# Two sequences' input rows and three sequences' output rows move by indirect DMAs from GpSimd, in a four-stage block on one core

## The chip, the core and the metric

The program runs on one core of a Trainium2 chip. The core has five instruction queues that run side by side: TensorE (PE), VectorE (DVE), ScalarE (ACT), GpSimd (POOL) and SyncE (SP), which here does nothing but issue DMAs. The metric is the device time of one execution in microseconds (us), the median of several runs; lower is better. Each engine works its own instructions off in the order in which they were written, and waits where one of them needs a result that isn't there.

## The reference

The input x is four sequences of 512 tokens with 256 features each. Four layers follow each other; each normalises x, computes something of it and adds that to x:

```python
x = L0_attn_a_x                                   # (4, 512, 256), float32
x = x + _L0_attn_a_ref(_layernorm(x), ...)        # stage m: convolution, then a selective scan over 512 tokens
x = x + _L0_ffn_ref(_layernorm(x), ...)           # stage e: 8 experts, the best two of each token weighed, RMS norm
x = x + _L0_attn_b_ref(_layernorm(x), ...)        # stage s: state-space layer of 64 heads, in chunks of 32 tokens
x = x + _L0_ffn_ref(_layernorm(x), ...)           # stage f: the expert layer again, same weights
return x
```

What matters for the change is only where x comes from and where it goes: all of x is read from the chip's memory (HBM) at the start, it stays in the on-chip memory (SBUF) through all four stages, and the sum after the last stage is written back. All numbers are float32.

## The kernel before

**Tiling.** A sequence of 512 tokens lies in SBUF as 128 partitions x 4 blocks x 256 features: the tile `x[b]` is `[P, NT, D]` with P = 128 and NT = 4, and token `i*128 + p` of sequence b is row p of block i. So one sequence is 512 KB, and each of its blocks 128 KB, 1 KB in each partition. There are four such tiles, one for each sequence, and they are never moved.

**Stages.** Within a stage the sequences follow each other, and the stages overlap at their seams: while the scans of the last sequence run, the expert layer of the first has begun, and so on. By the trace the stage of the scans (m) takes some 340 us, the expert layer (e) and the state-space layer (s) lie between 250 and 735 us, and the last expert layer (f) ends the run.

**The order of the work** is not the order of the Python code. All operations are noted first, as nodes with their inputs and outputs, by `Plan.note`. `price` gives each node a cost. `Plan.order` then simulates the engines: at each step it takes, on the engine that can start soonest, the node with the lowest rank among those that could start within 0.1 us of the earliest. `Plan.backward` gives the ranks: it schedules everything from the end backwards, and a node's rank is the latest time at which it may start by that. `Plan.issue` does both 24 times, replays each order with two sets of randomly lengthened costs, and keeps the order with the shortest replay. Then the instructions are written out in that order, all from line 611. So a change of one node's engine or cost may move any other instruction. Three details bear on the change: a DMA may not be issued more than 80 us ahead of its rank (`lead`); a DMA occupies its issuing queue for a fraction of a microsecond and a modelled transfer engine for its bytes at 360 GB/s (`Plan.run`, line 500); and the end that the replay minimises is the last instruction's end on its engine, without the landing of a DMA.

**The start.** `load(b)` (line 755) reads a sequence with one DMA of 512 KB from SP's queue. Sequence 0 is loaded first, then the weights of stage m come, sequences 1 to 3 between them. GpSimd meanwhile writes the constants: the identity `ident`, masks, `spread`, `less_all` and others, by memsets and selects. `measured(b)` (line 1174) computes the mean and variance of each row of `x[b]` on DVE (`st_m`, `mv_m`), and GpSimd raises the variance to the power -0.5 (`scale_m`).

**The end.** In stage f, `experts` (line 975) computes the experts of one block of 128 tokens: TensorE multiplies into `ph_f`, DVE adds the bias, ACT applies silu, DVE and ACT weigh the results into `cm_f`, `c_f` and `hb_f`, and GpSimd adds these: `c_f <- c_f,hb_f` and two adds `cm_f <- cm_f,c_f`. `project` (line 1011) transposes `cm_f` on TensorE (`pc_f`) and multiplies it with the projection (`pj_f`). `finish` (line 1033) takes the inverse root of the mean square on GpSimd (`rs_yf`), multiplies on DVE, and adds the result to x: by one GpSimd add of 128x1024 for a whole sequence (sequences 0, 1 and 2), or by one DVE add of 128x256 for each block (sequence 3, whose four blocks are finished one by one). Then SP writes the finished part to `out`: one DMA of 512 KB for each of the first three sequences, four of 128 KB for the last.

Of the kernel before, what the change touches and what calls it, by code (L numbers as in the profile page):

```python
# [30 lines left out]
P = 128  # L31
B, L, D = 4, 512, 256
NT = L // P
# [174 lines left out]
class Plan:  # L208
# [29 lines left out]
    def note(self, eng, op, args, kw):  # L238
# [2 lines left out]
        n.outs, n.ins = [], []  # L241
        first = True
        for k, v in [(None, v) for v in args] + list(kw.items()):
            if not isinstance(v, bass.AP):
                continue
            if k in ("out", "accum_out") or (k is None and first):
                n.outs.append(v)
            else:
                n.ins.append(v)
            if k is None:  # L250
                first = False
# [222 lines left out]
    def run(self, n, s, clock):  # L474
# [21 lines left out]
        if n.port:  # L496

            s = max(s, clock["port_of"].get(n.eng, 0.0))
            clock["port_of"]["vector" if n.eng == "gpsimd" else "gpsimd"] = s + c
        if n.dma:  # L500
            n.end = s + 0.06
            clock[n.eng] = n.end
            t = max(n.end, clock["hwdge"])
            clock["hwdge"] = t + 0.45
            n.end = clock[n.eng] = t + 0.4
            t = max(t + 0.45 + 0.65, clock["dma"])
            clock["dma"] = n.done = t + n.cost
            return
# [66 lines left out]
            self.emit(n)  # L575

    def swap(self, v):
        if not isinstance(v, bass.AP):
# [62 lines left out]

def price(plan, n):

    n.table, n.port, n.dma = None, False, n.op == "dma_start"
    out = n.outs[0]

    def place(ap):
# [69 lines left out]
def block(ctx: ExitStack, tc: Plan, a: dict, out: bass.AP):  # L717
# [5 lines left out]
    def ctile(shape, name):  # L723
        return const.tile(shape, F32, tag=name, name=name)

    def ctile_r(shape, name):
        return const.tile(shape, F32R, tag=name, name=name)

# [23 lines left out]
    for b in range(B):  # L752
        x.append(ctile([P, NT, D], f"x{b}"))

    def load(b):
        nc.sync.dma_start(out=x[b], in_=a["x"][b].rearrange("(i p) d -> p i d", p=P))

    load(0)
# [153 lines left out]
    def moe(name, w, where, sums, biased=lambda b: (), last=False):  # L912
# [120 lines left out]
        def finish(b, y, ss, lo=0, hi=NT):  # L1033
# [2 lines left out]
                V.scalar_tensor_tensor(y[:, i, :], y[:, i, :], ry[:, i - lo : i - lo + 1], norm_w, ALU.mult, ALU.mult)  # L1036
            some = x[b][:, lo:hi, :]
            (V if last and hi - lo == 1 else G).tensor_tensor(some, some, y[:, lo:hi, :], ALU.add)
            if last:
                nc.sync.dma_start(out=out[b, lo * P : hi * P, :].rearrange("(i p) d -> p i d", p=P), in_=some)  # L1040

        def steps(seqs, ahead=False):
# [960 lines left out]
```

## Time and profile before

| what | value |
|---|---|
| median of 3 runs | 843.76 us (838.05 to 845.73) |
| profiled execution | 838.11 us, its span 836.4 us |
| TensorE clock granted, mean | 0.883 of full speed |
| PE busy | 717.4 us (86%) |
| DVE busy | 683.8 us (82%) |
| POOL busy | 525.5 us (63%), 410 instructions |
| ACT busy | 523.4 us (63%) |
| loads of x (SP, 4 of 512 KB) | issued between 1.3 and 6.2 us |
| stores of sequences 0, 1, 2 (SP, 512 KB each) | 2.9 us from issue to landing (median) |
| stores of sequence 3 (SP, 4 of 128 KB) | 1.7 us from issue to landing (median) |

The span runs from the first to the last instruction; the execution's own time is 1.7 us longer, which lies around it. Busy times are shares of the whole span; the engines take turns at being the one that everything waits for. An instruction's name in the profile is `out<-in` by the program's tile names, the letter behind the underscore is the stage (m, e, s, f), and line 611 is where all of them are written out. `SPq` is the queue of DMAs that SyncE issues. Instructions that only issue DMAs aren't counted as busy time of an engine.

### The profile page before, as it was taken

To read this page: it belongs to the slowest core of one execution; us is meant where nothing else is said; L and a number is where in the kernel's file an instruction comes from. 1 tells how busy PE (TensorE), PEld (TensorE's weight loads), DVE (VectorE), ACT (ScalarE), POOL (GpSimd) and SP (SyncE) were. 2 spreads that over 40 slices of the span, in tenths; PEclk is the share of its full clock that TensorE was granted. 3 is DMA by queue.
4 is the path that set the end of the run, shared out by engine and by line. 5 is a ranking of instruction groups with operands and counts; after the bars stand their busy time and mean duration, and the time that the engine had idled before them with its cause. 6 is when DMAs were issued, how large, how long until landed. Compare 5 with 4: busy or idle time off the path is not lost. (4 is left out here: it accounts for less than half of the span.)

```text
span 836.4 us, 16364 instructions
## 1 busy us (share of the span) xinstructions
PE 717.4 (86%) x6160; PEld 460.4 (55%) x6160; DVE 683.8 (82%) x1272; ACT 523.4 (63%) x960; POOL 525.5 (63%) x410
## 2 busy tenths in 40 slices
PE   5997887977667799899998887888979888999996
PEld 2332323312013346687886666676668666878884
DVE  5439999999999994898998569785688567699987
ACT  2777875675335685678676646727736546576764
POOL 5714776776776774755558766771962864647755
PEclk9999998977569599999998678799969967999998
DMA  7362351441252101700002553431440574000101
GB/s 231 99 201 73 101 165 38 131 144 58 84 164 79 48 7 49 282 1 0 1 1 52 119 125 63 95 77 31 104 100 15 121 289 100 2 1 1 51 1 52
DMA packets 80175, 70.18 MB, mean 84 GB/s; under 512 B 48856, under 2 KB 66200, under 8 KB 79328
## 3 DMA queue, kind: packets, MB, share of 16 engines
q1 hardware_dynamic: 78624, 67.98, 28.2%
q10 hardware_dynamic: 1472, 1.15, 0.4%
q8 instruction: 49, 0.80, 0.4%
q14 instruction: 30, 0.25, 0.1%
HBM read 51.77 MB, written 17.32 MB: 83 GB/s over the span
## 5 line engine op out<-in xcount | busy, mean ns | idle before, releaser
L611 POOL TENSOR_TENSOR hs<-hs,cb 128x1024 f32<-128x1024 f32 x64 | 153.0, 2394 | 82.3 <-DVE hs L611 62.7
L611 DVE TENSOR_TENSOR_SCAN hs<-da,bx 128x512 f32<-128x512 f32 x128 | 150.9, 1206 | 2.7 <-ACT da L611 2.2
L611 ACT ACTIVATE da<-ds,a_neg 128x512 f32<-128x512 f32 x128 | 87.6, 689 | 87.0 <-DVE hs L611 83.7
L611 PE MATMUL ys<-hs,over 128*32 128x512 f32 x256 | 75.6, 737 | 29.9 <-POOL hs L611 29.9
L611 DVE TENSOR_TENSOR bx<-us,pb 128x1024 f32<-128x1024 f32 x64 | 76.1, 1200 | 9.6 <-DMA us<-u_rows 9.3
L609 ACT ACT_TABLE_LOAD x50 | 64.2, 1283 | 0.9
L611 PE MATMUL pconv<-hh,conv 128*128 128x512 f32 x128 | 61.5, 629 | 3.0 <-DVE st_m L611 1.6
L611 POOL TENSOR_TENSOR m_s<-m_s,gm_s 128x512 f32<-128x512 f32 x32 | 45.6, 1431 | 28.3 <-ACT m_s L611 27.4
L611 ACT ACTIVATE ph_e<-ph_e 128x512 f32<-128x512 f32 x64 | 36.9, 586 | 25.3 <-DVE ph_e L611 16.6
L611 ACT ACTIVATE ph_f<-ph_f 128x512 f32<-128x512 f32 x64 | 37.1, 588 | 23.6 <-DVE ph_f L611 23.4
L611 PEld LDWEIGHTS ys<-hs,over 128*32 128x32 f32 x256 | 9.3, 116 | 68.7 <-POOL hs L611 56.4
L611 DVE TENSOR_TENSOR ph_f<-ph_f,expert_b 128x512 f32<-128x512 f32 x64 | 44.0, 692 | 2.7 <-PE ph_f L611 2.1
L611 PE MATMUL ph_e<-expert_h,xs_of_xh_e 128*128 128x512 f32 x128 | 43.8, 411 | 2.7 <-ACT c_e L611 2.7
L611 PEld LDWEIGHTS pconv<-hh,conv 128*128 128x128 f32 x128 | 24.4, 198 | 35.9 <-issue 31.0
L611 DVE TENSOR_TENSOR_SCAN starts<-decays_s_p,starts 128x1024 f32<-128x1024 f32 x16 | 39.9, 2497 | 3.7 <-ACT starts L611 3.7
L611 PE MATMUL pz_s<-x_b,m_s 128*32 128x32 f32 x2048 | 33.4, 218 | 10.4 <-DMA x_b<-x_rows_s 6.3
L611 PEld LDWEIGHTS pz_s<-x_b,m_s 128*32 128x32 f32 x2048 | 27.3, 128 | 25.8 <-issue 16.9
L611 PE MATMUL pe_s<-c_s,less 128*128 128x512 f32 x64 | 32.9, 563 | 9.5 <-DMA less<-cs_rows_s 7.8
L611 ACT COPY starts<-pst_s_p 128x512 f32<-128x512 f32 (+1 forms) x32 | 30.0, 1008 | 15.6 <-PE pst_s_p L611 15.6
L611 DVE TENSOR_TENSOR m_s<-pe_s,gm_s 128x512 f32<-128x512 f32 x32 | 21.8, 681 | 21.1 <-ACT pe_s L611 13.3
L611 PE MATMUL ph_f<-expert_h,xh_f 128*128 128x512 f32 x96 | 38.3, 399 | 0.3 <-ACT xh_f L611 0.3
L611 PE MATMUL ph_f<-expert_l,xh_f 128*128 128x512 f32 x96 | 38.4, 400 | 0.0
(389 smaller groups left out, 2153.7 us busy)
## 6 DMA issues: line engine op xcount, KB each, us to landing
ds<-d_rows SPq DMA_DIRECT2D x16, 512.0 KB, 3.8
us<-u_rows SPq DMA_DIRECT2D x16, 512.0 KB, 4.4
decays_s_p<-dk_rows_s SPq DMA_DIRECT2D x32, 256.0 KB, 4.1
cb<-c_rows SPq DMA_DIRECT2D x16, 256.0 KB, 3.5
x_rows_s<-xw_s SPq DMA_DIRECT2D x16, 256.0 KB, 2.4
x_b<-x_rows_s SPq DMA_DIRECT2D x64, 64.0 KB, 2.9
x<-in_x_dram SPq DMA_DIRECT2D x4, 512.0 KB, 7.7
raw_expert<-in_expert_w_dram SPq DMA_DIRECT2D x4, 512.0 KB, 6.4
```

The costliest lines, as they stand in the source:

```text
L609: self.real.scalar.preload_act_table_set(n.table)
L611: n.inst = f(*[self.swap(v) for v in n.args], **{k: self.swap(v) for k, v in n.kw.items()})
```

## The change

A table `tokens` of 128 x 16 integers is written by one GpSimd instruction (`iota`): column `b*4 + i` holds the token numbers `(b*4 + i)*128 + p` of block i of sequence b, counted over all 2048 tokens. Sequences 2 and 3 are then loaded by four indirect DMAs each, one for each block of 128 rows (128 KB), whose rows are named by a column of the table; and sequences 0, 1 and 2 are stored by four indirect DMAs each, again a block of 128 rows at a time. GpSimd issues all twenty. Sequences 0 and 1 are loaded, and sequence 3 is stored, by SP as before. The rows that move are the same as before. The planner learns of the new kind: such a DMA holds GpSimd for 1.3 us and begins to move data 1.0 us later.

```diff
@@ Plan.note
+            if isinstance(v, bass.IndirectOffsetOnAxis):
+                v = v.ap
@@ Plan.run
+        if n.dma and n.eng == "gpsimd":
+            n.end = clock[n.eng] = s + 1.3
+            t = max(n.end + 1.0, clock["dma"])
+            clock["dma"] = n.done = t + n.cost
+            return
         if n.dma:
@@ price
-    n.table, n.port, n.dma = None, False, n.op == "dma_start"
+    n.table, n.port, n.dma = None, False, n.op in ("dma_start", "indirect_dma_start")
@@ block
+    tokens = ctile_i([P, B * NT], "tokens")
+    G.iota(tokens, pattern=[[P, B * NT]], base=0, channel_multiplier=1)
+
+    def rows_of(b, i):
+        return bass.IndirectOffsetOnAxis(ap=tokens[:, b * NT + i : b * NT + i + 1], axis=0)
+
     def load(b):
+        if b > 1:
+            for i in range(NT):
+                G.indirect_dma_start(
+                    out=x[b][:, i, :], out_offset=None, in_=a["x"].rearrange("b t d -> (b t) d"), in_offset=rows_of(b, i)
+                )
+            return
         nc.sync.dma_start(out=x[b], in_=a["x"][b].rearrange("(i p) d -> p i d", p=P))
@@ finish
-            if last:
+            if last and hi - lo > 1:
+                for i in range(lo, hi):
+                    G.indirect_dma_start(
+                        out=out.rearrange("b t d -> (b t) d"), out_offset=rows_of(b, i), in_=x[b][:, i, :], in_offset=None
+                    )
+            elif last:
                 nc.sync.dma_start(out=out[b, lo * P : hi * P, :].rearrange("(i p) d -> p i d", p=P), in_=some)
```

The rest of the diff lets the planner's `swap` replace the table's tile inside such an argument, as it does for other tiles.

More of the change, by code (lines that the diff above doesn't have):

```diff
@@ L577, in swap @@
     def swap(self, v):
+        if isinstance(v, bass.IndirectOffsetOnAxis):
+            return bass.IndirectOffsetOnAxis(ap=self.swap(v.ap), axis=v.axis)
         if not isinstance(v, bass.AP):
@@ L724, in ctile, with ctile_i @@
         return const.tile(shape, F32, tag=name, name=name)
+    def ctile_i(shape, name):
+        return const.tile(shape, mybir.dt.int32, tag=name, name=name)
     def ctile_r(shape, name):
```

## The prediction

> **What bounds the kernel now.** I read the page's slices first, then the busy time of each engine in four stretches where the change touches GpSimd, then GpSimd's instructions in order of time at both ends, then the chain that ended last. The slices of GpSimd say that it is nowhere full.
>
> ```profile
> POOL 5714776776776774755558766771962864647755
> PEclk9999998977569599999998678799969967999998
> ```
>
> The stretches hold, after their total, the busy time of PE, weight loads, DVE, ACT and POOL, then the granted clock, the DMA share and GB/s.
>
> ```profile
> 0.00:47.00 47.00, 37.25 (x84) 14.80 (x84) 23.26 (x81) 25.92 (x41) 27.34 (x47) 1.00 0.56 173
> 640.00:700.00 60.00, 50.47 (x963) 38.82 (x961) 36.58 (x72) 32.25 (x56) 36.76 (x32) 0.82 0.64 182
> 760.00:800.00 40.00, 40.00 (x218) 33.80 (x217) 36.38 (x96) 28.20 (x69) 27.47 (x23) 1.00 0.08 27
> 800.00:837.00 37.00, 28.16 (x139) 22.83 (x138) 29.13 (x77) 20.55 (x51) 20.89 (x22) 0.93 0.09 29
> ```
>
> In the first 47 us GpSimd is busy for 27.3 and so idle for 19.7. In 760 to 800 TensorE is full (40.00 of 40), DVE has 91%, and GpSimd idles for 12.5. In the last 37 us TensorE has only 28.2: the run ends with a chain through all engines, block by block of sequence 3. From 640 to 700 TensorE idles for 9.5 us while the DMA engines are at 64%: there the weights of stage f are read back.
>
> Here is GpSimd at the very end (start, duration, tiles, and in brackets the idle time before):
>
> ```profile
> 818.66 1.29 POOL L611 TENSOR_TENSOR c_f<-c_f,hb_f 128x512 f32<-128x512 f32 x1 [1.80 <-ACT hb_f L611]
> 821.75 1.63 POOL L611 TENSOR_TENSOR cm_f<-cm_f,c_f 128x256 f32<-128x256 f32 x2 [1.80 <-DVE cm_f L611]
> 823.33 2.37 POOL L611 TENSOR_TENSOR x<-x,xnb_f 128x1024 f32<-128x1024 f32 x1
> 825.66 1.28 POOL L611 TENSOR_TENSOR c_f<-c_f,hb_f 128x512 f32<-128x512 f32 x1
> 827.01 1.55 POOL L611 TENSOR_TENSOR cm_f<-cm_f,c_f 128x256 f32<-128x256 f32 x2
> 828.52 1.09 POOL L611 TENSOR_TENSOR rs_yf<-sd_yf,minus_half 128x1 f32<-128x1 f32 x2
> 830.14 0.72 POOL L611 TENSOR_TENSOR rs_yf<-sd_yf,minus_half 128x1 f32<-128x1 f32 x1 [0.53 <-DVE sd_yf L611]
> 832.07 0.72 POOL L611 TENSOR_TENSOR rs_yf<-sd_yf,minus_half 128x1 f32<-128x1 f32 x1 [1.21 <-DVE sd_yf L611]
> ```
>
> From 821.75 to 832.79 it is hardly idle, and the chain that ended last runs through it (start, length, engine and tile):
>
> ```profile
> 823.38 2.33 POOL x L611
> 825.71 1.24 POOL c_f L611
> 827.01 0.75 POOL cm_f L611
> ```
>
> The add of 128x1024 at 823.3 is the last step of sequence 2 (`finish`). It has nothing to do with sequence 3, but sequence 3's `c_f` add stands behind it. So, at the place where sequence 2's results leave, GpSimd itself is what the end waits for. That is the one place where more GpSimd work must cost something.
>
> **What is removed.** Five DMAs leave SP's queue: two loads of x, three stores.
>
> ```profile
> L611 SPq DMA_DIRECT2D out_dram<-x x7: 332/350/400, 778.9 to 833.8; - x7
> L611 SPq DMA_DIRECT2D x<-in_x_dram x4: 368/476/507, 1.3 to 6.2; - x4
> ```
>
> At 0.35 us for a store and 0.48 for a load (the middle figures of min/median/max) that is 2.0 us of SP. At the start SP issued the loads of sequences 2 and 3 at 5.83, and `dt_w` stood behind them at 8.09; but `dt_w` is first read at 39.6, so nothing is gained by its coming 2 us earlier. At the end nothing but sequence 3's own stores stands behind sequence 2's, and these were waiting for DVE. I count 0, and at most 2.0 gained.
>
> **What is added.** One `iota`, eight gathers and twelve scatters on GpSimd's queue. No indirect DMA is in this trace. By kind the nearest row is SP's issue of the same 128 KB, 0.35 us; by engine it is GpSimd's largest piece of work, 2.4 us for 128x1024. I take 1.3: the add of 128x512 on GpSimd takes 1.29, and the new plan is computed with 1.3, so its order fits if that is right. For the landing I take the row of the stores of 128 KB, 1.7 us after the issue, and up to 8.7, the longest landing of any transfer of x. For `iota` I take the 0.3 us of a select of 128x128.
>
> *The start.* 8 x 1.3 + 0.3 = 10.7 us, against 19.7 idle before 47 us; at 2.4 it would be 19.5, just as much as there is. A gather waits for nothing but the table, so it blocks nothing behind it by waiting, only by its 1.3 us. Behind it in GpSimd's queue stand the powers `scale_m`, the first of which is on the way to the first convolution: it ended at 14.39 and DVE used it at 16.29, so 1.9 us of delay are free and one gather in front of it is covered. The rows of sequences 2 and 3 are read by DVE at about 20 us. If they come late, DVE stands still, as it works in order; before its next urgent work (`b_s` at 37.8) it had 9.1 us idle, which covers seven more microseconds of gathers. That cover is gone if one costs over 2.4 us. The same 1 MB now competes from a second queue with the convolution's weights, which TensorE awaited until 9.64. Together +0.5 us, with bounds 0 and +3 (the 1.3 us of one gather in front of a power and 1.7 for one late landing).
>
> *Sequences 0 and 1.* 8 x 1.3 = 10.4 us of GpSimd in the 40 us after 776 us or so, where it has 12.5 idle; TensorE is full there and what it multiplies next (`ph_f`) doesn't come from GpSimd, only `pc_f` does, a few times. A scatter waits for the add in front of it on the same engine, so nothing else is held up by the wait, but each may hold a `c_f` or `cm_f` add by up to 1.3 us. +1 us. Bounds: 0, and 8 x 2.4 - 12.5 = +6.7, if the issue is that long and all of the excess reaches TensorE.
>
> *Sequence 2.* 4 x 1.3 = 5.2 us. After its add ended at 825.7, GpSimd had 7.1 us to the end of its last power at 832.79, 5.4 of them busy: 1.7 are free. 3.5 are too many. Behind the last power they would put the last issue at 836.3 and its landing at 838.0, where the last store of sequence 3 was issued at 833.8 and, with 1.7 us, landed at 835.5: +2.5. But the planner may also pull sequence 2 forward: its power was ready at 813.0, DVE's multiplies of it were spread from 815.8 to 822.0, and GpSimd idled for 4.4 us between 813 and 823 (0.8 + 1.8 + 1.8). Then the add leaves the end's chain. I take +2; bounds 0 and 4 x 2.4 = +9.6.
>
> **Sum** 0 + 0.5 + 1 + 2 = +3.5, between -2.0 and +19.3. Against the profiled execution's 838.11 (span 836.4, and 1.7 around it) that is 841.6. That execution is 5.65 below the median of the runs, 843.76, so the median to expect is 847.3; I say 847. The three runs lie 0.9% apart; about 1% is what a measurement of this kernel can tell from no change.
>
> **A rule that speaks against the change.** The trace shows DVE standing still because of GpSimd:
>
> ```profile
> 23.78 2.59 DVE L611 TENSOR_SCALAR sd_m<-mv_m 128x4 f32<-128x4 f32 x4
> 23.78 2.38 POOL L611 TENSOR_TENSOR expert_l<-raw_expert,expert_h 128x1024 fp32r<-128x1024 f32 x1 [2.07 <-ACT expert_h L611]
> ...
> 39.65 0.16 DVE L611 TENSOR_SCALAR scale_m<-scale_m 128x4 f32<-128x4 f32 x1
> ```
>
> Four instructions of 128x4 take 2.59 us on DVE in the 2.38 us in which GpSimd subtracts 128x1024; later one such takes 0.16 us. The Trainium skill (SBUF — State Buffer, "Who interferes with whom") has this the other way round too: a DMA issued from GpSimd needs descriptors that GpSimd writes through the port it shares with DVE, and a DVE instruction in a two-port mode keeps it out until it ends. No transfer of this trace is issued by GpSimd, so no row shows that. By the rule gathers beside DVE's copies at the start would be the late ones; its example is 3.1 us in place of 0.62, and by that eight would be up to 20 us late (an estimate from that page). At the end DVE works mostly out of TensorE's result memory. My sum doesn't use this; it goes by the bounds above.
>
> **The rivals.**
>
> *Absorbed, a little slower* (47%): as summed, 847.
>
> *The issue is dear* (20%): a gather or scatter holds GpSimd for 2.4 us. For: an add of 128x1024 takes that long, and how long it takes to write out 128 rows' addresses no row shows. Against: the adds of 128x256, the tile that such a DMA moves, take 0.75. Then the middle costs up to 6.7, the end four times 1.1 more than above (6.4), the start 3: +16, or 860. It decides from 12.5 / 8 = 1.6 us an issue upward, where the eight no longer fit into the idle time.
>
> *The new order is worse in the middle* (21%): since one node's cost changes all ranks, the order of everything is new. The place that is sensitive is 671 to 687: 5 MB of weights were put ahead of small transfers on SP's queue, the chain has 13.4 us of `expert_h` there, and TensorE idled for 9.5 us of those 60. A like mistake once more costs some 9.5: 843.8 + 9.5 = 853. Against it: the planner tries 24 orders.
>
> *The new order is better there* (12%): the same 9.5 us won, with the 3.5 of the sum: 838. To pass the bound of 1% below it must also win the 1.3 us by which sequence 2's add held `c_f` and a little more, 835.
>
> **How the numbers follow.** 847 is the likeliest. Slower by over 1% (above 852) are the two slower cases, 41%, less the part of them that stays below: 39%. Faster by over 1% (below 835) is most of the last case, 11%. Within 1% is the rest, 50%. A range of 8 in 10 leaves out the lower half of the last case and the upper half of the dear issue: 838 to 860.
>
> **What would show it.** Right: gathers in GpSimd's gaps before 47 us and the first scan on DVE at about 63.8 us as before; TensorE still full from 760 to 800; scatters issued 1 to 1.6 us apart; the last GpSimd work after sequence 2's add 2 to 5 us longer than before. Wrong: an issue far from 1.3; DVE idle before `st_m` of sequence 3; another stretch between 60 and 760 that is longer or shorter by more than all of this, which would be the order's doing and not the DMAs'.

## The result, and the profile after

The changed kernel takes **876.03 us** (median of 4 runs, 872.16 to 877.39); the kernel before, measured beside it, 844.75 (838.05 to 845.85). The ratio is **1.038**, with a 95% interval of 1.0316 to 1.0444. The forecast was 847, its range 838 to 860. The profiled execution of the changed kernel took 876.33 us, its span is 874.6, against 836.4 before: 38.2 us more to explain. By the medians it is 31.3; the profiled execution of before was a short one, so some 7 of the 38.2 are chance.

All instructions are now written out at line 620, and everything in the middle lies some 20 us later. The page's slices of GpSimd and of the granted clock:

```profile
POOL 7814876767765675645466867547734657466755
PEclk9998999977667699899997799698688769999996
```

GpSimd is still nowhere full, so it has not become the engine that bounds the whole. The granted clock is 0.875 in the mean; before it was 0.883. The stretches answer to those of before (total; PE, weight loads, DVE, ACT, POOL; granted clock, DMA share, GB/s); the third and fourth are moved by 20 us:

```profile
0.00:47.00 47.00, 34.74 (x75) 13.95 (x75) 18.59 (x80) 20.14 (x33) 35.26 (x55) 0.96 0.51 158
660.00:720.00 60.00, 50.33 (x909) 40.04 (x909) 29.71 (x54) 30.69 (x54) 36.87 (x31) 0.78 0.65 177
780.00:820.00 40.00, 37.19 (x187) 30.80 (x186) 33.43 (x81) 24.79 (x59) 28.74 (x26) 0.96 0.05 17
820.00:875.00 55.00, 36.60 (x175) 29.03 (x174) 39.07 (x91) 25.19 (x62) 31.67 (x33) 0.84 0.08 27
```

GpSimd has 35.26 us in the first 47 instead of 27.34, which is about the eight gathers: unlike SP's issues, an indirect DMA is counted as busy time of GpSimd here (55 instructions instead of 47). The second row, around the reload of stage f's weights, has as much of TensorE as before (50.33 and 50.47 of 60). In the third row TensorE was full before (40.00 of 40); now it has 37.19. The end, 37 us before, is 55 us long, and TensorE is busy for 36.6 of it. The transfers themselves, from the profile's view of the tile `x` (duration of the issue, not of the transfer; min/median/max in ns, first and last start):

```profile
L620 POOL DMA_INDIRECT out_dram<-x,tokens x12: 960/1012/1083, 794.9 to 868.2; - x12
L620 POOL DMA_INDIRECT x<-in_x_dram,tokens x8: 947/987/1433, 1.9 to 22.2; - x8
L620 SPq DMA_DIRECT2D out_dram<-x x4: 356/370/405, 862.9 to 871.6; - x4
L620 SPq DMA_DIRECT2D x<-in_x_dram x2: 454/476/499, 1.3 to 1.8; - x2
```

An issue of an indirect DMA takes 0.99 to 1.01 us in the median. SP keeps two loads and sequence 3's four stores, at what they cost before. Twenty issues are 20 us of GpSimd, of which much had idle time to lie in; so their price is not what explains 38 us. What does, at the end, is seen in GpSimd's order of time at the end (start, duration, tiles, idle time before and what ended it):

```profile
794.92 1.08 POOL L620 DMA_INDIRECT out_dram<-x,tokens  x1 [0.17 <-POOL c_f L620]
797.70 0.96 POOL L620 DMA_INDIRECT out_dram<-x,tokens  x1 [1.70 <-DMA out_dram<-x,tokens]
...
821.80 0.99 POOL L620 DMA_INDIRECT out_dram<-x,tokens  x1
826.08 0.96 POOL L620 DMA_INDIRECT out_dram<-x,tokens  x1 [3.29 <-DMA out_dram<-x,tokens]
827.07 1.29 POOL L620 TENSOR_TENSOR c_f<-c_f,hb_f 128x512 f32<-128x512 f32 x1
...
865.40 1.04 POOL L620 DMA_INDIRECT out_dram<-x,tokens  x1 [2.94 <-DMA out_dram<-x]
868.16 0.96 POOL L620 DMA_INDIRECT out_dram<-x,tokens  x1 [1.73 <-DMA out_dram<-x,tokens]
```

The scatters don't run freely behind the add. The second started 1.70 us after the first had been issued, and the releaser is the landing of the first; the third of the next sequence waited 3.29 us for the second, and `c_f <- c_f,hb_f` stood behind it. Every scatter names the whole of `out` as its destination, since only the table says which rows it writes; so the program orders each behind the one before. The stores of sequence 3 on SP's queue write to the same tensor, and are in the same chain: the scatter at 865.40 waited 2.94 us for one of them. The waits of SP's queue for scatters are (us in all, times, the longest):

```profile
SPq L620 <- DMA out_dram<-x,tokens: 148.6, 5, 98.7
```

Five waits, the longest of 98.7 us: SP comes to a store long before its data are there, so most of this costs nothing. At the very end it does cost. The chain that ended last (start, length, what) now goes through these transfers:

```profile
862.90 1.72 DMA out_dram<-x
...
865.40 1.04 POOL out_dram L620
...
869.14 0.59 POOL rs_yf L620
```

Before, its last 13 us were GpSimd's adds and the work of other engines on sequence 3; now a store of sequence 3, a scatter of sequence 2 that waits for it, and behind the last scatter the power of sequence 3's last block, 0.59 us. After TensorE's last instruction the changed kernel runs on for 12.3 us; before it was 5.7.

Three moments that are the same work in every version cut the span into stretches: the first scan of stage m on DVE, the last product `po_s` of stage s on TensorE, and the end. By them the 38.2 us of the two profiles fall into three parts:

| stretch (us) | before | after | more |
|---|---|---|---|
| start to the first scan | 63.8 | 67.0 | +3.2 |
| first scan to the last `po_s` | 667.1 | 683.7 | +16.6 |
| last `po_s` to the end | 105.5 | 123.9 | +18.4 |

No indirect DMA lies in the middle one. So there were two questions: what do the DMAs cost where they are, and what does the new order of everything cost?

### The profile page after: what moved, and what is told of

Its sections match the earlier page's. It is cut to its first block, busy times and chain, and to the rows that moved or that the text cites. A ratio compares the mean times of both kernels' runs of the same rounds, so it can differ in the third digit from the quotient of the medians.

```text
span 874.6 us, 16387 instructions
## 1 busy us (share of the span) xinstructions
PE 728.8 (83%) x6160; PEld 463.2 (53%) x6160; DVE 685.3 (78%) x1272; ACT 533.7 (61%) x969; POOL 544.0 (62%) x431
## 4 chain that ended last, share of the span: by engine, by line
PE 35%; DVE 12%; ACT 9%; issue 4%; SPq 4%; DMA 4%; POOL 2%; POOLq 0%; ACTq 0%; DVEq 0%
PE ph_e L620 7%; PE ph_f L620 6%; SPq L620 4%; PE po_s L620 3%; DVE hs L620 3%; PE pz_s L620 3%; ACT L618 3%; PE px_s L620 2%; PE pst_s_p L620 2%; PE po_s_p L620 1%; DMA decays_s_p<-dk_rows_s 1%; PE pe_s L620 1%; DVE bx L620 1%; PE pr_s L620 1%; PE pj_e L620 1%
## 5 line engine op out<-in xcount | busy, mean ns | idle before, releaser
L620 POOL TENSOR_TENSOR hs<-hs,cb 128x1024 f32<-128x1024 f32 x64 | 150.7, 2364 | 77.6 <-DVE hs L620 61.6
L620 PE MATMUL ys<-hs,over 128*32 128x512 f32 x256 | 84.6, 781 | 34.7 <-POOL hs L620 34.7
L620 PE MATMUL pconv<-hh,conv 128*128 128x512 f32 x128 | 59.0, 603 | 2.3 <-ACT hh L620 2.3
L620 PE MATMUL pz_s<-x_b,m_s 128*32 128x32 f32 x2048 | 33.2, 209 | 12.8 <-DMA x_b<-x_rows_s 7.0
L620 PE MATMUL ph_f<-expert_h,xl_f 128*128 128x512 f32 x96 | 38.9, 405 | 0.0
```

The lines of the kernel that those rows point to most:

```text
L620: n.inst = f(*[self.swap(v) for v in n.args], **{k: self.swap(v) for k, v in n.kw.items()})
```

## Experiments: the order and the DMAs taken apart

Theory O: most of the loss is the new order. Theory D: most of it is the DMAs themselves. They can be parted, because the order is planned first and written out after: one can plan with one kind of DMA and write out the other.

**Before's order with the indirect DMAs** (`old_order_indirect`). The plan is before's, instruction by instruction on each engine; where a load of sequence 2 or 3 or a store of sequence 0, 1 or 2 comes up, four indirect DMAs are written out on GpSimd instead.

```diff
+        if "rows" in n.kw:                       # a load of 2, 3 or a store of 0, 1, 2
+            b = n.kw["rows"]
+            for i in range(NT):
+                at = IndirectOffsetOnAxis(ap=tokens[:, b*NT+i : b*NT+i+1], axis=0)
+                g.indirect_dma_start(...)        # gather into x[b][:, i, :], or scatter from it
+            return
```

> The plan of the kernel before is kept for all engines; only where it issued the loads of sequences 2 and 3 and the stores of sequences 0, 1 and 2 from SP, four indirect DMAs of GpSimd stand in GpSimd's queue instead. If the new order of everything is what costs (theory O: about 20 of the 31 us were lost before stage f began, in stretches that hold no indirect DMA): 855 to 862, the loss all in the first 50 us and after 776 us, because each block of four scatters holds GpSimd for about 4 x (1.0 issue + 1.7 wait for the scatter before) = 10.8 us and the last block stands in the end's chain. If the indirect DMAs themselves cost (theory D): 872 to 880, and the stretches between 130 and 640 us longer too.

Measured: 875.05 us (873.08 to 877.81), ratio 1.0384 (1.0316 to 1.0452). First scan at 72.5 (+8.7), middle stretch 668.1 (+1.0), end 133.8 (+28.3). The order is before's, and yet all of the loss is there. Theory D's time is met; its other half, longer stretches between 130 and 640 us, is not, as the whole middle is 1.0 us longer.

**The new order with plain DMAs** (`new_order_plain`). The plan is the changed kernel's; at each of the twenty places SP issues a plain DMA of the same 128 KB.

```diff
+        if n.op == "indirect_dma_start":
+            b, i = n.kw["rows"]
+            rows = slice(i * P, (i + 1) * P)
+            if n.kw["in_offset"] is None:
+                sync.dma_start(out=out[b, rows, :], in_=n.kw["in_"])
+            else:
+                sync.dma_start(out=n.kw["out"], in_=x[b, rows, :])
+            return
```

> The order of the changed kernel is kept for all engines; each of the twenty indirect DMAs is a plain DMA of the same 128 KB from SP. Theory O: 862 to 868 (stage f begins 20 us late as in the changed kernel, and what the scatters cost after that, 8 to 12, is gone). Theory D: 843 to 849, as the kernel before.

Measured: 858.21 us (853.83 to 860.39), ratio 1.0168 (1.0101 to 1.0235), beside 842.05 for before. First scan at 64.1, middle stretch 684.2 (+17.1), end 110.4 (+4.9). No DMA is indirect, and half of the loss is there: less than theory O's 862 to 868, more than theory D's 843 to 849.

**The new order, scatters that don't wait** (`new_order_spare`). As the changed kernel, but each of the twelve scatters writes to a buffer of its own; the output of sequences 0, 1 and 2 is left unwritten.

```diff
-                        out=out.rearrange("b t d -> (b t) d"), out_offset=rows_of(b, i), in_=x[b][:, i, :], ...
+                        out=a["spare"][NT * b + i], out_offset=rows_of(0, 0), in_=x[b][:, i, :], ...
```

> The order of the changed kernel is kept; the twelve scatters write to twelve buffers of their own, which are nobody's result (sequences 0, 1 and 2 of the output are not written), so no scatter waits for the one before it to land. If the waits between scatters (10.1 us of GpSimd's idle time in the profile) are what stage f lost: 864 to 869, with stage f some 85 us long as before and the tail after the last expert multiply near 15 us. If the issue time of 1.0 us is what hurts: 873 to 877, no change.

Measured: 862.01 us (861.13 to 865.39), ratio 1.0244 (1.0179 to 1.0309). The end is 113.0. The waits' theory had 864 to 869, 2 us more; that of the issue time had 873 to 877, and falls.

**What follows.** Neither theory was right alone, and the loss of the changed kernel comes apart in its own order:

| version | us | ratio to before | step |
|---|---|---|---|
| before, in this set of runs | 842.05 | 1 | |
| the changed kernel's order, plain DMAs | 858.21 | 1.0168 | the order: 16.2 us, by the ratio 14 |
| the same, indirect DMAs, none waits for another | 862.01 | 1.0244 | twenty issues on GpSimd: 3.8, by the ratio 6 |
| the changed kernel | 876.03 | 1.038 | the waits of one write to `out` for another: 14.0, by the ratio 11 |

(The last was measured in another set, where before had 844.75, so the ratio is the better guide there; the profiles put the end at 123.9 and 113.0, 10.9 apart.) Twenty issues cost 4 to 6 us by the medians: about what the prediction had worked out, 3.5. This step is the least certain of the three: the single runs lie apart (853.83 to 860.39, and 861.13 to 865.39), but the two ratios' intervals overlap. The other 25 to 30 us are two things that the sum had left out; one of them, the order, stood beside it as a rival. Theory D's time for before's order was right for a reason of its own: there all four scatters of a sequence stand in a row, and all eight gathers too, so the DMAs cost 33 us by themselves.

## Experiments: what the DMAs cost, in before's order

These keep before's order on every engine, so that only the DMAs differ. (Beside the runs from here on, before had medians of 841.86 to 842.72.) Their forecasts speak of theory W (the scatters cost by what is queued behind them, mostly in their waits), theory S (it was the late start's doing), theory H (it is GpSimd's time for the issues) and theory L (the gathers' rows come too slowly).

**Only the scatters, in a row** (`old_order_scatters`): the edit of `old_order_indirect` for the stores alone.

> The order of before, instruction by instruction; only the stores of sequences 0, 1 and 2 are four scatters each, in a row on GpSimd where SP's store was issued. No gathers. In the run with all twenty DMAs in this order, the last x<-po_s to the end took 133.5 us instead of 105.2: +28.3. Theory W (the scatters cost by holding up what is queued behind them on GpSimd, each for about 1.0 us of its own and 1.7 us of wait for the one before): first scan at 63.8, end +28, so 866 to 874 us. Theory S (much of that end was the late start's and the gathers' doing): end below +15, under 858.

Measured: 872.55 us (867.85 to 874.66), ratio 1.0365 (1.0322 to 1.0408); end 132.2, +26.7. GpSimd after the add of sequence 1:

```profile
796.65 2.37 POOL L628 TENSOR_TENSOR x<-x,xnb_f 128x1024 f32<-128x1024 f32 x1 [1.28 <-DVE xnb_f L628]
798.98 1.28 POOL L628 TENSOR_TENSOR c_f<-c_f,hb_f 128x512 f32<-128x512 f32 x1
800.43 1.04 POOL L642 DMA_INDIRECT out_dram<-x,tokens  x1 [0.17 <-POOL c_f L628]
803.18 0.96 POOL L642 DMA_INDIRECT out_dram<-x,tokens  x1 [1.70 <-DMA out_dram<-x,tokens]
805.85 0.96 POOL L642 DMA_INDIRECT out_dram<-x,tokens  x1 [1.71 <-DMA out_dram<-x,tokens]
```

**The same, to separate buffers** (`old_order_scatters_spare`; the output of sequences 0 to 2 is left unwritten).

```diff
-                    out=out.rearrange("b t d -> (b t) d"), out_offset=at, ...
+                    out=self.spare[NT * b + i], out_offset=IndirectOffsetOnAxis(ap=tokens[:, 0:1], axis=0), ...
```

> As the run before, but the twelve scatters write to twelve separate 128 KB buffers, so none waits for another (the output of sequences 0 to 2 is left unwritten). The waits are gone and the issues, 12 of about 1.0 us, stay. Theory W: the block of four holds GpSimd some 4.5 to 5 us instead of 9 to 10.7, so the end grows by 8 to 15 instead of 28: 850 to 858 us, and the step between the two runs is 14 to 20. Theory H (it is GpSimd's time for the issues, not the wait): within 4 us of the run before.

Measured: 852.3 us (851.09 to 855.46), ratio 1.0129 (1.0088 to 1.017); end 118.3, +12.8. The same place:

```profile
793.49 1.04 POOL L643 DMA_INDIRECT spare<-x,tokens  x1 [0.17 <-POOL c_f L628]
794.84 0.96 POOL L643 DMA_INDIRECT spare<-x,tokens  x1 [0.30 <-PE ph_f L628]
796.10 0.96 POOL L643 DMA_INDIRECT spare<-x,tokens  x1 [0.30 <-issue]
```

In the first fence a scatter starts every 2.7 us, with 1.70 to 1.72 idle before it; in the second every 1.3, with 0.30. The step between the two runs is 20.3 us, at the upper end of theory W's 14 to 20. The block of four holds GpSimd for 9.0 us in the one and 4.8 in the other, and nearly all of it reaches the end: 26.7 is three times 8.9, and 12.8 three times 4.3. How it gets there is seen in what TensorE waits for: `pc_f`, the transpose of `cm_f`, has to wait for GpSimd's adds (us in all, times, the longest). In the kernel before, with the scatters in a row, and with separate buffers:

```profile
PE pc_f L611 <- POOL cm_f L611: 0.4, 1, 0.4
PE pc_f L628 <- POOL cm_f L628: 22.1, 3, 9.5
PE pc_f L628 <- POOL cm_f L628: 10.4, 3, 5.3
```

So it doesn't help that GpSimd has 12.5 us idle in the 40 us of that place: the idle time lies in gaps of at most 4 us, and a block that is longer than the gap it starts in makes the `c_f` and `cm_f` adds late, and TensorE with them.

**The gathers, put into the gaps** (`gathers_placed`). Only the gathers of sequences 2 and 3; two in front of the first power `scale_m`, six behind it.

```diff
+    def before_pool(self, n):
...
+            if n.eng == "gpsimd" and any(s.startswith("scale_m") for s in names):
+                self.flush(2)                    # two gathers
+                self.flushing = True
...
+    def after_pool(self, n):
+        if self.flushing and self.later[0][0]:
+            self.flush(6)                        # the others
```

> The order of before; only the loads of sequences 2 and 3 are gathers, and they stand in GpSimd's idle time: two in front of the first power scale_m, six behind it. Stores by SP. Theory W (in the run with all eight in a row in front of that power, the power came 8.6 us late and with it the first scan): first scan at 63.8 to 66, so 841 to 846 us. Theory L (the gathers' rows come too slowly, or their traffic holds up the weights): first scan still at 70 or later, 848 to 852.

Measured: 842.8 us (839.78 to 847.02), ratio 1.0006 (0.998 to 1.0033). They cost nothing that these runs could tell from no change. The first scan is at 63.8, as before; that it agrees to the tenth is chance, since `old_order_spread`, with the gathers in the same places, has 66.0 (its granted clock from 20 to 30 us was 0.83, here 1.00), and the two runs of scatters, with before's own loads, have 62.3 and 63.0. GpSimd's order of time shows why. In `old_order_indirect` all eight stand in front of the power:

```profile
5.59 1.39 POOL L620 DMA_INDIRECT x<-in_x_dram,tokens  x1 [0.30 <-POOL tokens L616]
...
14.81 0.95 POOL L620 DMA_INDIRECT x<-in_x_dram,tokens  x1 [0.30 <-issue]
...
21.30 1.69 POOL L629 TENSOR_TENSOR scale_m<-sd_m,minus_half 128x8 f32<-128x8 f32 x1
```

In `gathers_placed` the same instructions are:

```profile
12.66 1.69 POOL L628 TENSOR_TENSOR scale_m<-sd_m,minus_half 128x8 f32<-128x8 f32 x1
14.54 1.02 POOL L638 DMA_INDIRECT x<-in_x_dram,tokens  x1 [0.19 <-issue]
...
21.87 1.68 POOL L628 TENSOR_TENSOR scale_m<-sd_m,minus_half 128x8 f32<-128x8 f32 x1
```

The power is at 21.30 in the one and at 12.66 in the other (12.73 before). The gathers behind it took the time that GpSimd spent waiting until 20.05 in the kernel before. DVE did wait for the rows, 3.5 us in all at `st_m`; that was covered.

**All twenty, each scatter with other work behind it** (`old_order_spread`). The gathers as in the last run; the scatters of sequences 0 and 1 with at least 1.7 us of GpSimd's own work (by the planner's costs) between one and the next, those of sequence 2 with one instruction between.

```diff
+        if not load:
+            self.flush(1)                        # the first scatter at once
...
+        self.since += n.cost                     # after each instruction of GpSimd
+        if self.since >= (0.6 if rows == 2 else 1.7):
+            self.flush(1)
```

> All twenty indirect DMAs and the order of before, but each scatter of sequences 0 and 1 is put one or two GpSimd instructions (1.7 us or more of work) behind the one before, so that its wait is spent on other work; those of sequence 2 follow the add with one instruction between each; the gathers stand as in the run with the placed gathers. Theory W: start 0 to +3; the first eight cost 8 x 1.0 in GpSimd's idle time, 0 to +4; sequence 2's four cost 4 x 1.0 and some 2 of wait on the last chain, +6: 846 to 856 us, faster than the changed kernel by 20 to 30. Theory H: 12 issues and 8 gathers cost their full time, 860 to 866.

Measured: 852.5 us (850.31 to 852.91), ratio 1.0113 (1.0074 to 1.0152). This is the whole change, 23 us faster than the changed kernel, and 10 slower than before. GpSimd at the second and third stores of sequence 0:

```profile
790.79 2.42 POOL L628 TENSOR_TENSOR x<-x,xnb_f 128x1024 f32<-128x1024 f32 x1
793.38 0.99 POOL L642 DMA_INDIRECT out_dram<-x,tokens  x1 [0.17 <-issue]
794.39 1.32 POOL L628 TENSOR_TENSOR c_f<-c_f,hb_f 128x512 f32<-128x512 f32 x1
796.09 0.98 POOL L642 DMA_INDIRECT out_dram<-x,tokens  x1 [0.38 <-DMA out_dram<-x,tokens]
```

The wait for the scatter's landing is spent on an add, and 0.38 us are left of it. By the adds of x that end each sequence (their start after the last `po_s`), the cost of a sequence's stores is seen one by one:

| after the last `po_s` (us) | before | in a row | to separate buffers | spread |
|---|---|---|---|---|
| add of sequence 1 | 53.5 | 62.8 | 58.6 | 54.5 |
| add of sequence 2 | 92.4 | 109.0 | 99.3 | 95.0 |
| end | 105.5 | 132.2 | 118.3 | 114.2 |
| so the stores of 0 and 1 cost | | 16.6 | 6.9 | 2.6 |
| and those of 2 | | 10.1 | 5.9 | 6.1 |

Spread out, eight scatters cost 2.6 us although they still wait for one another. Sequence 2's four, with one instruction between, stay on the path: they stand between its add and the last work of sequence 3. Theory W holds in all four runs; S fell with the first, H with the second, L with the third.

## Experiments: what a new order costs

The order is half the loss. Theory A: the planner was misled, by pricing each scatter's bytes as the whole output and by not knowing the waits, and reckons its order worse (its replay gives 866.6 us for the changed kernel's order and 857.6 for before's); an order is worth what it reckons. Theory B: every new order is a draw, and before's is a lucky one. Theory C: ACT's table loads, 60 in the changed kernel and 50 in before, set the middle.

**Another order of before** (`before_other_pick`): the random numbers of the replay are drawn anew (`random.Random(2)` for `random.Random(1)`), and with them the planner takes the fifteenth of its 24 orders, not the sixteenth.

> The kernel before with no indirect DMA at all, but another seed of the planner's replay costs, so that it picks another of its 24 orders. Theory O (orders that the planner holds for equally good differ by one or two per cent on the chip): between 838 and 870, outside of 840 to 849 more likely than not. Theory D: 840 to 849, since nothing is changed that moves data.

Measured: 845.92 us (843.41 to 850.18), ratio 1.0048 (1.002 to 1.0076). The middle stretch is 676.6, 9.5 longer; an earlier first scan (60.4) takes 3.4 of that back. The time lies in theory D's range, 840 to 849, where theory O held it less likely than not to lie.

**The gathers alone** (`gathers_only`) and **the scatters alone** (`scatters_only`), each with the planner's own order; the other edit of the change is left out.

> The table and the eight gathers of sequences 2 and 3 alone; all stores by SP as before; the planner makes its own order. Theory A (the gathers are covered by GpSimd's idle time at the start, and it is the scatters that spoil both the order and the end): the planner's replay of this order, 857.4, equals that of before, 857.6, so 836 to 848 us, first scan within 4 us of before's 63.8, from the last scan on nothing longer. Theory B (any new order is a draw, worse by some 15 us as often as not, whatever moved the ranks): a middle (first scan to the last x<-po_s) of 667 to 685 us, 842 to 860. Theory C (ACT's table loads set the middle: 50 in before, 54 in the other pick, 60 in after): this order has 42, so 834 to 841.

> The table and the twelve scatters alone; all loads by SP as before; the planner's own order. Theory A: the planner itself puts this order at 865.3 against 857.6, because twelve scatters with nothing behind them crowd GpSimd's ranks at the end: middle +8 to +17, last x<-po_s to the end +18 as in the changed kernel, so 866 to 878 us. Theory B: middle anywhere between 667 and 685, end +18: 858 to 876. Theory C: 48 table loads, so a middle as in before, and only the end is longer: 858 to 862.

Measured: gathers 847.18 us (844.1 to 850.77), ratio 1.0062 (1.0032 to 1.0091); scatters 863.95 us (862.37 to 867.18), ratio 1.0266 (1.0214 to 1.0318). The middle stretches are 674.7 and 680.4. So with the gathers alone, which the planner reckons as good as before, the middle is 7.6 longer too: not what theory A or C forecast. The total stays within theory A's, as the first scan is 2.5 earlier. The scatters alone are 2 us under theory A's 866 to 878 and above theory C's 862; theory B's ranges take in both runs.

**The planner told of the waits** (`planner_told`).

```diff
-            n.end = clock[n.eng] = s + 1.3
+            n.end = clock[n.eng] = s + 1.0
+        if n.op == "indirect_dma_start":
+            b = 4 * P * D                        # the bytes that move
+        if op == "indirect_dma_start" and kw["in_offset"] is None:
+            n.preds.update(self.wrote[-1:])      # a scatter waits for the one before
+            self.wrote.append(n)
```

> All twenty indirect DMAs, but the planner is told three things that the trace of the changed kernel showed: a scatter waits for the landing of the scatter before, its bytes are 128 KB (not the whole output), and it holds GpSimd for 1.0 us. Its replay is 859.4 against 866.6 of the changed kernel's order and 857.6 of before's; 46 table loads. Theory A (the planner spoiled its order because it priced the scatters wrongly): a middle within 4 us of before's 667, an end of 110 to 118 us instead of 123.5, so 848 to 860 us. Theory B: middle 667 to 685, so 850 to 876. Theory C: middle as in before or shorter, 846 to 856.

Measured: 859.69 us (858.92 to 861.74), ratio 1.022 (1.0174 to 1.0266). The end is 115.3 instead of 123.9, as theory A had it, and the time is at the upper end of A's range, but the middle is 676.7, and not within 4 of before's 667.1.

**One unused instruction** (`before_unused_iota`): the kernel before with the table's `iota`, which nothing reads.

> The kernel before with one more instruction, the table's iota, which nothing reads: 0.15 us of GpSimd, but new ranks and so another order (replay 860.4 against 857.6; 52 table loads). Theory A: the replay tells the order's worth, so 843 to 848 us. Theory B: a draw, 838 to 860, with a change of over 1% as likely as not. Theory C: two more table loads, 842 to 845.

Measured: 849.22 us (845.63 to 856.8), ratio 1.0105 (1.0067 to 1.0142). An instruction of 0.15 us made the kernel 1% slower, by more than theories A and C allow (848 and 845). It did so by the new order: the middle stretch, long after it, is 680.6.

**Other orders of the two kernels.** Two more of before's 24 orders and two more of the changed kernel's:

```diff
-            if best is None or last < best[0]:
+            if turn == 6:                        # 7; 9 and 11 for the changed kernel
```

> The kernel before, with another of its own 24 orders: the seventh, which the planner reckons at 803.6 us and its replay at 866.1; that is what it reckons for the changed kernel's order (803.1 and 866.6). No indirect DMA. Theory A (the planner's reckoning tells an order's worth, and the change costs because it leaves the planner with a worse one): as the changed kernel's order with plain DMAs, 853 to 863 us, the stretch from the first scan to the last x<-po_s 680 to 687. Theory B (each order other than before's is a draw between 667 and 685 in that stretch, whatever is reckoned): 843 to 860, anywhere.

> As the run before with the eighth order, reckoned at 797.8, replay 864.3. Theory A: between before and the run above, 850 to 857. Theory B: 843 to 860, and not necessarily ordered by the replay.

> The changed kernel with another of its 24 orders: the tenth, reckoned at 792.0 us with a replay of 872.1 (the one taken has 803.1 and 866.6); 48 table loads. Theory A by the replay: 5 us slower than the changed kernel, 878 to 886; by the model without the replay's lengthened costs: 11 us faster, 862 to 868. Theory B: the stretch from the first scan to the last x<-po_s between 667 and 685, so 858 to 878.

> The changed kernel with the twelfth of its orders, reckoned at 798.2 us with a replay of 868.6; 50 table loads. Theory A by the replay: 2 us slower than the changed kernel, 876 to 880. Theory B: 858 to 878.

Measured, with what the replay reckons by before's random numbers:

| order | table loads planned | replay | middle stretch | measured us | ratio |
|---|---|---|---|---|---|
| before | 50 | 857.6 | 667.1 | 842 | 1 |
| `before_other_pick` | 54 | 862.3 | 676.6 | 845.92 | 1.0048 (1.002 to 1.0076) |
| `before_turn_7` | 52 | 864.3 | 676.1 | 848.68 | 1.0088 (1.005 to 1.0126) |
| `before_turn_6` | 52 | 866.1 | 673.3 | 843.67 | 1.0023 (0.9996 to 1.0049) |
| the changed kernel | 60 | 866.6 | 683.7 | 876.03 | 1.038 (1.0316 to 1.0444) |
| `after_turn_11` | 50 | 868.6 | 676.4 | 860.55 | 1.0217 (1.0172 to 1.0263) |
| `after_turn_9` | 48 | 872.1 | 671.0 | 857.29 | 1.0178 (1.0135 to 1.0221) |

Theory A falls. The order of before that is reckoned like the changed kernel's, 866.1, is 0.2% slower than before (an interval that takes in no change), where the changed kernel's order with plain DMAs is 1.7% slower; this comparison is a loose one, as the 866.6 holds what the planner charges for the indirect DMAs. But of the changed kernel's three orders, all planned with the same charges, the one that the planner took as the best is the slowest, by 1.6 to 2.0% of before's time (14 to 17 us). Theory C falls too: with 42 table loads `gathers_only` has a middle of 674.7, with 46 `planner_told` 676.7. What is left is theory B. Over the eleven different orders that were run, the middle stretch goes from 667.1 to 683.7 us. Before's order, in the six profiles that have it, gives 667.1 to 671.6, and of the ten others only `after_turn_9`, with 671.0, comes so low; the changed kernel's is the longest of all. The five other orders without scatters (one of them with the gathers) are 1.8 to 7.0 us slower than before in the median, 4.9 in the mean; the changed kernel's order with plain DMAs is 16.2 slower. A change that makes the planner start anew gives up the first and draws another, and this one drew the worst of those that were run.

Why this order is longer could be followed only a little way. Here are the two longest parts behind the scans, from the last scan of stage m to the last `ph_e` and from there to the last scan of stage s, in the kernel before (columns as above):

```profile
310.90:436.60 125.70, 119.13 (x591) 94.19 (x592) 104.88 (x285) 86.08 (x191) 70.75 (x64) 0.99 0.15 56
436.60:707.60 271.00, 232.11 (x4102) 178.62 (x4101) 194.52 (x334) 156.78 (x283) 171.41 (x142) 0.83 0.41 100
```

And in `new_order_plain`:

```profile
314.80:453.60 138.80, 131.19 (x645) 103.30 (x645) 111.90 (x302) 94.54 (x208) 77.05 (x68) 0.98 0.16 54
453.60:716.70 263.10, 215.49 (x3888) 166.83 (x3887) 178.51 (x298) 150.22 (x266) 163.08 (x137) 0.82 0.41 99
```

TensorE is idle for 38.9 us of the second part before (271.00 less 232.11) and for 47.6 in the new order, and for about 1 us more in the first. Over the whole middle stretch its idle time goes from 98.9 to 112.0, and its busy time, at much the same granted clock, from 568.3 to 572.5. So two thirds of the added idle time lie in stage s, as many small waits; no single one of them is over 8 us in sum. Which decision of the planner made them stays open.

## Why the prediction was wrong

**What is removed** (0): nothing spoke against it.

**The price of an issue** (1.3, bounds 0.35 to 2.4): right. A scatter holds GpSimd for 1.01 us, a gather for 0.99 (medians), and two in a row stand 1.26 apart, with 0.30 between. `iota` took 0.15 us, not 0.3. The rival of the dear issue (2.4) is out.

**The landing** (1.7 us after the issue): about right as the sum used it, from the issue's end: a scatter lands 1.4 to 1.5 us after that, and 1.70 to 1.72 pass until the next one, which waited for it, starts. The row that it was taken from counts from the issue's start; counted so, a scatter takes 2.4 to 2.5, and that the figure fitted is luck. The Trainium skill (DMA: Bandwidth & Descriptors, "Anatomy of one DMA — SWDGE (gpsimd) path") gives a fit of 2.0 us and the bytes at 436 GB/s for such a transfer; 128 KB would be 2.3 us by that, and the runs have 2.4 to 2.5 from issue to landing.

**The start** (+0.5, bounds 0 and +3): the mechanism was named, and it is not shown that its size was far off. The first scan came 3.2 us later. The planner put five gathers in front of the first power, from 1.9 us on, and there the rows of sequences 2 and 3 move beside the convolution's weights. This is TensorE's long run of `pf` on the second part of these weights (before: from 9.64) in the changed kernel (start, duration, tiles, idle time):

```profile
11.31 6.96 PE L620 MATMUL pf<-conv_w,in_x 128*128 128x512 f32 x12 [2.94 <-DMA conv_w<-in_conv_w_dram]
```

And in the same order with plain DMAs, `new_order_plain`:

```profile
8.29 8.14 PE L628 MATMUL pf<-conv_w,in_x 128*128 128x512 f32 x14 [0.25 <-DMA conv_w<-in_conv_w_dram]
```

The weights came 3.0 us later, and not because of GpSimd's time: TensorE waits for their DMA. In all six runs that gather from 1.9 us on, it idles for 2.5 to 2.9 us there. But little of that reaches the first scan. `new_order_spare` has the same order and the same gathers:

```profile
10.71 3.78 PE L620 MATMUL pf<-conv_w,in_x 128*128 128x512 f32 x4 [2.63 <-DMA conv_w<-in_conv_w_dram]
```

There the first scan is at 64.8, only 0.7 later than with plain DMAs (64.1) and 1.0 later than before. Of the other 2.1 us of the changed kernel's 67.0 most arose later, between 28 and 42 us, when no gather is issued; from 37 to 43 us its granted clock was 0.72, that of `new_order_spare` 1.00. These are single profiles, so the gathers' price at the start is some 1 to 3 us. The cover that I named for GpSimd's time is there: placed from 10.2 us on, the gathers cost nothing.

**Sequences 0 and 1** (+1): here is **the first step that failed**: "A scatter waits for the add in front of it on the same engine, so nothing else is held up by the wait". I looked for what a scatter reads and not for what it writes. All twelve write to one tensor, at rows that only the table knows, so each waits for the one before. In the changed kernel's order the first eight cost 7.0 us against plain DMAs (add of sequence 2 at 100.9 after the last `po_s`, not 93.9), and 1.3 us with separate buffers. So the 12.5 us of idle time did cover the issues in this order (in a row, in before's order, the same eight cost 6.9); they didn't cover waits that a scatter spends at the head of GpSimd's queue. Of the signs that the prediction named, scatters 1 to 1.6 us apart and a TensorE that stays full from 760 to 800 did not come: two that follow each other directly start 2.7 us apart, and TensorE has 37.19 us of the 40 from 780 on.

**Sequence 2** (+2, bounds 0 and +9.6): 6.5 us in the changed kernel (the end 13.5 longer than with plain DMAs, less those 7.0), within the bounds. Without waits it was 1.4. Much of it lies behind TensorE's last instruction: 12.3 us in the changed kernel, 6.7 without waits and 5.9 with plain DMAs.

So the waits, which have no term in the sum, are worth 11 to 14 us by the changed kernel and `new_order_spare`, which differ only in where the scatters write.

**The new order worse in the middle** (21%, +9.5): this is **the second step that failed**: the sum counted it at nothing. The prediction did name a longer stretch between 60 and 760 us as the sign of it, and that came (+16.6). I took the order as it stood to be as good as the next, and the planner's 24 tries as a reason against a loss. The runs say the opposite: none of ten other orders beats the order before. So the rival "new order better" should have had little chance, and a mean draw, +4.9, belonged into the sum itself (no run before the change had shown it); the draw that came cost 14 to 16, more than the 9.5 of the rival. That the reload of weights at 671 to 687 would be the place was not shown: the loss is spread over stage s.

With the waits (11 to 14) and a mean draw (4.9) the sum would have been 19 to 22, and the forecast 863 to 866. The changed kernel's two other orders and that of the planner that was told of the waits, 857 to 861, lie on the near side of that; the changed kernel's own lies 10 to 13 beyond it.

**The rule of the Trainium skill** that was weighed (SBUF — State Buffer, "Who interferes with whom"). The row first: the issues took 0.95 to 1.43 us while DVE worked beside them, and in the run with the gathers placed DVE waited 3.5 us in all for their rows. By an example of the same page ("A bandwidth-pool intuition that's wrong (but worth ruling out)") the prediction put eight gathers at up to 20 us late, as its estimate; nothing like it is in these runs. They don't show how long the writing of descriptors was kept waiting, so the rule isn't refuted either. What the traces show again is the other direction, of which the prediction had a row: a DVE instruction of 128x32 that takes 0.18 us elsewhere stood still for 4.37 us, until GpSimd had finished its add:

```profile
826.41 4.37 DVE L620 TENSOR_TENSOR r_f_f<-lg_f,r_m_f 128x32 f32<-128x32 f32 x1
...
828.31 2.42 POOL L620 TENSOR_TENSOR xnb_f<-xnb_f,moe_rows 128x1024 f32<-128x1024 f32 x1
```

The first part of this fell beside the scatter's issue (826.08 to 827.04); whether the scatter alone would hold DVE up is not shown. The instruction stands on the chain of the last 75 us. In the same order with plain DMAs the longest of the eight such instructions takes 1.62 us; here the third scatter, late by its wait, had moved `c_f` and the add of 128x1024 onto it.

## To carry to other kernels

Ask of a DMA that is moved not only what it reads but what it writes: scatters into one tensor at rows named by a table follow one another, each until the one before has landed (here 1.7 us at the head of the queue each time, 11 to 14 us in all, against 4 to 6 for the issues), unless the destinations are separate or other work of that queue, longer than the landing, stands between them. Idle time of an engine covers a new instruction only if it lies in gaps that are as long as the instruction with its wait. And where a planner picks the order, look at how much its orders differ on the chip before counting a change at the sum of its instructions: if the order at hand is the best of many, a change that makes it plan anew is likely to pay the difference to a usual one.

## What the hardware showed that was not expected

- Two indirect DMAs in a row on GpSimd have 0.30 us between them, which the profile mostly puts down to issue; between a scatter and an add behind it there are only some 0.03 us.
- The gathers' time from issue to landing depends on when they are issued: 5.0 us in the median in the changed kernel, where they start at 1.9 us beside the first weights, and 3.5 where they are placed from 10.2 on; a scatter at the end, where the DMA engines are at 5 to 8%, takes 2.4 to 2.5.
- Orders of the same instructions, all built by the same rules, lie up to 16.6 us apart in the stretch between the first scan and the last `po_s`, 2.5% of it; one unused instruction of 0.15 us, by the new order it brought, moved the kernel by 1%.
